# GpSimd's next operation made to depend on a mask or weight-split pass of VectorE, in a cross-attention layer with layer norm

## The chip, the cores and the metric

The kernel runs on one core of a Trainium2 chip. The metric is the device time of one execution in microseconds: before the change the median of 3 runs is 513.0 us (512.81 to 514.88). A core has five engines that work side by side, each through its own queue of instructions in order: TensorE (PE; its weight loads are shown apart as PEld), VectorE (DVE), ScalarE (ACT), GpSimd (POOL) and SyncE (SP), which here only issues DMAs. Engines wait for each other by semaphores. An instruction that waits holds up everything behind it in its engine's queue.

## What is computed

Four sequences of 2048 rows attend to 77 context rows each, 16 heads of 32; the output projection, the residual and a layer norm follow. Everything is float32, and the mask drops the last context rows.

```python
qs = (q @ wq).reshape(Bq, Lq, H, HD).transpose(0, 2, 1, 3)
ks_ = (k @ wk).reshape(Bq, Lk, H, HD).transpose(0, 2, 1, 3)
vs = (v @ wv).reshape(Bq, Lk, H, HD).transpose(0, 2, 1, 3)
scores = jnp.einsum('bhqd,bhkd->bhqk', qs, ks_) / jnp.sqrt(jnp.float32(HD))
scores = jnp.where(mask[:, None, :, :], -jnp.inf, scores)
attn_w = jax.nn.softmax(scores, axis=-1)
attn = jnp.einsum('bhqk,bhkd->bhqd', attn_w, vs)
attn = attn.transpose(0, 2, 1, 3).reshape(Bq, Lq, H * HD)
out = attn @ wo + q
mu = jnp.mean(out, axis=-1, keepdims=True)
var = jnp.mean((out - mu) ** 2, axis=-1, keepdims=True)
return (out - mu) / jnp.sqrt(var + EPS) * gamma + beta
```

## The kernel before

The 8192 rows are 64 tiles of 128 (numbers t), 32 blocks of two tiles (b) and 16 groups of four (g). Large products are made of three passes over values that are split into a rounded part and a rest (`xth` and `xtl`, `wqh` and `wql`, `AH` and `AL`), so a rest has to be computed by a subtraction for each operand.

The order of the whole kernel is written out by hand: the string ORDER is a list of words, and a loop at the end of the kernel issues one step per word. A word is a letter and a number, with a part behind a dot. Each engine gets its instructions in the order of the words; there is no scheduler behind it. Waits are derived from the data: an instruction waits for those that write what it reads, or still use what it overwrites. The words that matter here, with their engine and line:

- VectorE: `F` (L356) and `G` (L368) subtract a rounded weight from the loaded weight, for the value and the output weights, 4 of each; `M` (L386) turns mask bytes into an additive bias, 17 passes, of which M28.4 is that of tiles 28 to 31 and M44.4 that of tiles 44 to 47. All three read and write SBUF alone. `T` (L420) takes the maxima of four heads out of the score banks, `r` (L445) the reciprocal of the sums, `t` (L471) transposes the probabilities, `q` (L290) moves queries out of PSUM, `b` (L529) makes the rest of the attention output, `+` (L561) adds the residual, `s` (L575, L576) takes mean and variance.
- ScalarE: `e` (L435) exponentials of four heads, `i` (L266) rounds the input, `a` (L525) rounds the attention output, `k` (L590) scales a tile for the layer norm.
- GpSimd: `j` (L270) the rest of the input, `n` (L450) divides a tile's probabilities by their sums, `f` (L593) and `)` (L596) multiply by gamma and add beta, `v` (L581 to L584) four small operations that make scale and shift of two tiles out of mean and variance. A `P` word that ends in g is a DMA which GpSimd issues (L482).
- TensorE: `Q` queries, `B` values' projection, `S` scores, `V` probabilities by values, `O` output projection.

A tile goes S, T, e, r, n, t, then by DMA into the layout for V. The probability buffers are three (`pbuf`), the score banks rotate through the eight PSUM banks by a table. So a tile's maxima free the banks for a later tile's scores, and n of a tile has to be done before t can begin. Words that stand close in ORDER on different engines don't run at the same time: each engine comes to its word when its own queue does.

## Time and profile before

| | before |
|---|---|
| median of the runs | 513.0 us |
| the profiled execution | 513.14 us |
| its span, first to last instruction | 511.3 us |
| granted TensorE clock | 0.998 |
| HBM traffic over the span | 115 GB/s |
| VectorE transposes, 64 | 95.8 us busy, 1498 ns each |
| GpSimd's n, 63 | 142.3 us busy, 2261 ns each |
| GpSimd's f and ), 56 of each | 72.1 and 72.0 us busy, 1292 and 1289 ns each |
| GpSimd's j, 28 of one form | 67.4 us busy, 2408 ns each |

The profile shows one execution. Times in its rows are microseconds from the start of the span: a row of the timeline gives start, duration, engine, line, operation, the tiles written and read, and in brackets how long the engine sat idle before it and whose end released it. A group row gives the shortest, median and longest duration of a line's instructions in nanoseconds. A row of the windows gives a stretch, its length, and how much of it an engine was busy.

### The profile page before, as it was taken

The numbers are of one execution on the slowest core, as the hardware profiler recorded it, in microseconds if no ns is written. First come the engines' busy times: TensorE is split into PE (matmuls) and PEld (weight loads), VectorE is DVE, ScalarE is ACT, GpSimd is POOL, SyncE is SP. The second block draws the span as 40 slices with busy tenths as digits, with TensorE's granted clock in tenths as the row PEclk, the third lists the DMA queues.
The fourth block names the chain that finished last, engine by engine and source line by source line (L and its number), as shares of the span: only waits on it lengthen the run. The fifth ranks groups of instructions, "written<-read, shape, count | busy, mean of one in ns | idle before, by whom it ended". The sixth has DMA issues, their size and how long they took to land. (4 is left out here: it accounts for less than half of the span.)

```text
span 511.3 us, 20308 instructions
## 1 busy us (share of the span) xinstructions
PE 499.2 (98%) x6833; PEld 383.9 (75%) x6833; DVE 470.3 (92%) x2563; ACT 464.6 (91%) x2222; POOL 421.1 (82%) x387
## 2 busy tenths in 40 slices
PE   8998999999999999999999999999999999999994
PEld 6976777777777877777777777778777777777773
DVE  5799889988999989988989998999999999999997
ACT  6698999999999999998999999999999999989720
POOL 2556656876897999998898899898999899898896
PEclk9999999999999999999999999999999999999999
DMA  8954786878686986779877868787879677699655
GB/s 307 390 196 131 173 220 163 230 177 225 192 245 182 267 222 169 229 210 249 245 223 210 228 172 252 178 219 204 247 201 235 189 217 240 192 228 252 162 185 216
DMA packets 58781, 110.85 MB, mean 217 GB/s; under 512 B 9462, under 2 KB 11278, under 8 KB 58678
## 3 DMA queue, kind: packets, MB, share of 16 engines
q1 hardware_dynamic: 55222, 102.75, 72.0%
q0 software_dynamic: 2496, 5.77, 4.0%
q8 instruction: 54, 0.88, 0.8%
q10 hardware_dynamic: 960, 1.05, 0.8%
q14 instruction: 49, 0.40, 0.3%
HBM read 41.79 MB, written 16.78 MB: 115 GB/s over the span
## 5 line engine op out<-in xcount | busy, mean ns | idle before, releaser
L435 ACT ACTIVATE pbuf<-pbuf,nm 128x77 f32<-128x77 f32 x1024 | 352.7, 352 | 8.7 <-DVE nm L420 8.0
L435 ACT ACTIVATION_READ_ACCUMULATOR pbuf<-pbuf,nm 128x1 f32 x1024 | 197.1, 193 | 0.0
L420 DVE CUSTOM_DVE_ANT_0 pbuf<-sc,mb 128x77 f32<-128x77 f32 x1024 | 170.0, 231 | 6.4 <-PE sc L403 4.6
L450 POOL TENSOR_TENSOR pbuf<-pbuf,ri 128x1232 f32<-128x1232 f32 x63 | 142.3, 2261 | 34.8 <-DVE ri L445 29.6
L552 PE MATMUL po<-woh,AH 128*128 128x512 f32 x256 | 104.0, 406 | 0.1
L471 DVE STREAM_TRANSPOSE B<-pbuf 128x1280 f32<-128x1280 f32 x64 | 95.8, 1498 | 8.2 <-POOL pbuf L450 7.2
L276 PE MATMUL pq<-xth,wqh 128*128 128x512 f32 (+1 forms) x256 | 100.6, 393 | 0.9 <-DVE nm L420 0.6
L552 PE MATMUL po<-wol,AH 128*128 128x512 f32 x256 | 100.0, 391 | 0.0
L552 PE MATMUL po<-woh,AL 128*128 128x512 f32 x256 | 99.9, 390 | 0.0
L276 PE MATMUL pq<-xtl,wqh 128*128 128x512 f32 (+1 forms) x256 | 98.2, 383 | 0.0
L276 PE MATMUL pq<-xth,wql 128*128 128x512 f32 (+1 forms) x256 | 98.1, 383 | 0.0
L420 DVE DVE_READ_ACCUMULATOR2_ANT nm<- 128x1 f32 x1024 | 84.4, 82 | 0.0
L270 POOL TENSOR_TENSOR xtl<-xtf,xth 128x1024 fp32r<-128x1024 f32 x28 | 67.4, 2408 | 9.6 <-issue 4.8
L593 POOL TENSOR_TENSOR o<-o,gam 128x512 f32<-128x512 f32 x56 | 72.1, 1292 | 2.9 <-ACT o L590 2.7
L596 POOL TENSOR_TENSOR o<-o,bet 128x512 f32<-128x512 f32 x56 | 72.0, 1289 | 1.4
L403 PEld LDWEIGHTS sc<-kct,q 32*64 32x64 f32 x4096 | 51.8, 130 | 24.4 <-issue 11.5
L403 PE MATMUL sc<-kct,q 32*64 32x77 f32 x4096 | 61.7, 238 | 2.2 <-DVE q L290 1.6
L496 PE MATMUL pa<-PT,vsb 96*32 96x256 f32 x992 | 59.7, 382 | 0.0
L552 PEld LDWEIGHTS po<-woh,AH 128*128 128x128 f32 x256 | 48.0, 188 | 15.3 <-issue 3.8
L276 PEld LDWEIGHTS pq<-xth,wqh 128*128 128x128 f32 x256 | 48.1, 188 | 14.7 <-issue 2.1
L552 PEld LDWEIGHTS po<-woh,AL 128*128 128x128 f32 x256 | 48.1, 188 | 10.5
L276 PEld LDWEIGHTS pq<-xth,wql 128*128 128x128 f32 x256 | 48.1, 188 | 9.6
(99 smaller groups left out, 640.3 us busy)
## 6 DMA issues: line engine op xcount, KB each, us to landing
PT<-B SPq DMA_DIRECT2D x343, 128.0 KB
xtf<-xT SPq DMA_DIRECT2D x28, 512.0 KB
o<-x SPq DMA_DIRECT2D x56, 256.0 KB
out<-o SPq DMA_DIRECT2D x56, 256.0 KB
PT<-B POOLq DMA_DIRECT2D x25, 128.0 KB, 4.8
stage_a<-kin SPq DMA_DIRECT2D x4, 410.0 KB
xtf<-xT SPq DMA_DIRECT2D x4, 256.0 KB
wq_f<-wq SPq DMA_DIRECT2D x4, 256.0 KB
```

Of the source, the lines that this page charges most:

```text
L270: nc.gpsimd.tensor_tensor(l[:, c : c + 2], fx.pop((g, c)), xh[g][:, c : c + 2].bitcast(F32), ALU.subtract)
L276: nc.tensor.matmul(pq, w[:, c, m * P : (m + 1) * P], r[g][:, c, rs], start=(n == 0), stop=(n == 11))
L403: mm = nc.tensor.matmul(sc[j][r0 : r0 + SR, g * NK : (g + 1) * NK], qs[q, g, rs.start + r0 : rs.start + r0 + SR], kct[q, g, t // TPB, keys ...
L420: nc.vector.tensor_tensor_reduce(pb[:, h // 2, (h % 2) * NK : (h % 2 + 1) * NK], scs[t][j][:, g * NK : (g + 1) * NK], mb[:, t % TPB, keys_ ...
L435: nc.scalar.activation(pb[:, h // 2, (h % 2) * NK : (h % 2 + 1) * NK], pb[:, h // 2, (h % 2) * NK : (h % 2 + 1) * NK], AF.Exp, bias=nmax[t ...
L450: nc.gpsimd.tensor_tensor(pv, pv, rv.to_broadcast((P, NP, 2, NK)), ALU.mult)
L471: nc.vector.transpose(bt.rearrange("p c q r -> p q c r"), pbuf[t % NPB].rearrange("p q (c r) -> p q c r", c=5),)
L496: nc.tensor.matmul(pas[b, g // 2][HD * j : HD * (j + 1), (g % 2) * BLK : (g % 2 + 1) * BLK], vsb[:, 2 * b // TPB, h % 2, HD * (h // 2) : H ...
L552: nc.tensor.matmul(pos[t], a[:, c, rs], w[:, c, :], start=(first and c == 0 and n == 0), stop=(c == NC_D - 1 and n == 2),)
L593: nc.gpsimd.tensor_tensor(od[t], od[t], gam, ALU.mult)
L596: nc.gpsimd.tensor_tensor(od[t], od[t], bet, ALU.add)
```

## The change

The helpers now return their instruction. While the words of ORDER are issued, the last instruction of a word F, G or M is remembered; the first word j, n, f or ) behind it in ORDER gets a dependency on that instruction, and the memory is cleared. Nothing is computed otherwise and no instruction changes its place on any engine.

```diff
+    def wait_for(later, earlier, reason):
+        info = mybir.DependencyInfo(mybir.DependencyClass.Sync, mybir.DependencyReason.DATA)
+        tc.add_manual_dep(later.ins, earlier.ins.name, info, reason=reason)
...
+    shared = None
     for word in ORDER.split():
...
-            ops[op](int(k or 0), int(part or 0))
+            ins = ops[op](int(k or 0), int(part or 0))
+            if op in "FGM":
+                shared = ins
+            elif shared and op in "jnf)":
+                wait_for(ins, shared, "VectorE's pass over two tiles of SBUF is begun ahead of GpSimd's")
+                shared = None
```

There are 25 words F, G and M, and 16 dependencies, since several passes can stand ahead of one GpSimd word: j2 on M8.4, n0 on F0, j5 on F2, j7 on G0, n9 on M28.4, f2 on M16.4, n14 on M20.4, )2 on M24.4, n24 on M32.4, n30 on M36.4, n35 on M44.4, j23 on M40.4, n45 on M48.4, n47 on M52.4, f45 on M56.4 and )46 on M60.4. A dependency is a wait for the semaphore that VectorE counts up at the end of the pass.

The order in which the instructions stand is unchanged; what changes are the semaphores that GpSimd waits for. GpSimd from the division n35 (of tile 35, in `pbuf_82`) to f25, before:

```order
L450 TENSOR_TENSOR pbuf_82<-pbuf_82,ri_5018 128x8x154 [waits DVE_49]
L596 TENSOR_TENSOR o_4415<-o_4415,bet 128x512
L593 TENSOR_TENSOR o_4542<-o_4542,gam 128x512 [waits DMAHW6_49,Activation_49]
L270 TENSOR_TENSOR xtl_5178<-xtf_2_4894,xth_5008 128x1024 [waits DMAHW7_49,PE_49]
L593 TENSOR_TENSOR o_4530<-o_4530,gam 128x512 [waits Activation_49]
```

and with the change (the lines are 3 further down in the file):

```order
L453 TENSOR_TENSOR pbuf_82<-pbuf_82,ri_5018 128x8x154 [waits DVE_49,Activation_49]
L599 TENSOR_TENSOR o_4415<-o_4415,bet 128x512
L596 TENSOR_TENSOR o_4542<-o_4542,gam 128x512 [waits DMAHW6_49,Activation_49]
L270 TENSOR_TENSOR xtl_5178<-xtf_2_4894,xth_5008 128x1024 [waits DMAHW7_49,DVE_49,PE_49]
L596 TENSOR_TENSOR o_4530<-o_4530,gam 128x512 [waits Activation_49]
```

The fourth row, j23, has a new wait for VectorE (DVE_49). The first, n35, had one already, for the reciprocal `ri_5018`; it now waits for a later count of the same semaphore, that of M44.4, and for ScalarE's exponentials by name, for which the reciprocal stood before. VectorE's own rows from that reciprocal on, the same in both:

```order
L445 RECIPROCAL ri_5018<-sum_4911 128x16
L529 TENSOR_TENSOR AL_5035<-pa_0_4916,AH_5033 128x512
L471 STREAM_TRANSPOSE B_5038<-pbuf_81 128x8x5x32
L561 TENSOR_TENSOR o_4438<-po_5040,o_4438 128x512
L290 COPY q_5073<-pq_3_5060 128x512
L386 TENSOR_SCALAR mb_3681<-m_2_2585 128x384
L529 TENSOR_TENSOR AL_5035<-pa_1_4917,AH_5033 128x512
L471 STREAM_TRANSPOSE B_5038<-pbuf_82 128x8x5x32
```

Between the first row, which n35 waited for, and the sixth, M44.4, for which it waits now, stand four operations of VectorE; the eighth is t35, which waits for n35. The other place is GpSimd's )46 (`o_7660`, adding `bet`) with v24 and three DMA issues ahead of n58, before:

```order
L596 TENSOR_TENSOR o_7660<-o_7660,bet 128x512 [waits Pool_49]
L581 TENSOR_TENSOR rn_8203<-mv_8004,small 128x2 [waits DVE_49]
L582 TENSOR_TENSOR rn_8203<-rn_8203,small 128x2 [waits Pool_49]
L583 TENSOR_TENSOR rn_8203<-mv_8004,rn_8203 128x2 [waits Pool_49]
L584 TENSOR_TENSOR rn_8203<-rn_8203,small 128x2 [waits Pool_49]
L482 DMA PT_8143<-B_8058 32x2x512 [waits DMAHW2_49,DMASW2_49,DMAHW3_49,DMASW1_49,DMAHW6_49,DVE_49,PE_49]
```

and with the change:

```order
L599 TENSOR_TENSOR o_7660<-o_7660,bet 128x512 [waits DVE_49,Pool_49]
L584 TENSOR_TENSOR rn_8203<-mv_8004,small 128x2
L585 TENSOR_TENSOR rn_8203<-rn_8203,small 128x2 [waits Pool_49]
L586 TENSOR_TENSOR rn_8203<-mv_8004,rn_8203 128x2 [waits Pool_49]
L587 TENSOR_TENSOR rn_8203<-rn_8203,small 128x2 [waits Pool_49]
L485 DMA PT_8143<-B_8058 32x2x512 [waits DMAHW2_49,DMAHW3_49,DMASW2_49,DMAHW6_49,DMASW1_49,PE_49]
```

The wait for VectorE has moved from the later rows to )46 itself: M60.4 stands behind everything of VectorE that v24 and the first DMA waited for, so their own waits have gone.

## The prediction

> **What bounds the kernel now.** The first view is the page's busy times, the second the waits of TensorE (engine, what it ran, for whom it waited: us in total, times, longest).

> ```profile
> PE 499.2 (98%) x6833; PEld 383.9 (75%) x6833; DVE 470.3 (92%) x2563; ACT 464.6 (91%) x2222; POOL 421.1 (82%) x387
> PE sc L403 <- DVE q L290: 1.6, 2, 1.3
> PE pq L276 <- DVE nm L420: 0.6, 1, 0.6
> PE sc L403 <- DVE q L292: 0.4, 1, 0.4
> PE sc L403 <- DVE nm L420: 0.2, 1, 0.2
> ```

> TensorE is the bound, and it hardly waits: all that it loses to VectorE in the whole run is 1.6 + 0.6 + 0.4 + 0.2 = 2.8 us. That is the ceiling of any gain from VectorE alone. But the other two engines of the score loop are over 90% busy and are chained to each other by every tile (maxima, exponentials, GpSimd's division, transposition), so an in-order engine that is held for some microseconds has little room to hide it. Small gain, larger risk: the rest works out both.

> The third view is that of the passes on which the change hangs (ns: shortest, median, longest).

> ```profile
> L386 DVE TENSOR_SCALAR mb<-m x17: 204/354/2109, 18.3 to 446.5; 128x384 bf16<-128x384 uint8 x15, 128x96 bf16<-128x96 uint8 x1, 128x288 bf16<-128x288 uint8 x1
> L368 DVE TENSOR_TENSOR wol<-stage_b,woh x4: 673/683/2904, 32.9 to 44.3; 128x512 fp32r<-128x512 f32 x4
> ```

> A mask pass takes 0.35 us and once 2.11; a split takes 0.68 and once 2.90. Each stretched one began while a GpSimd operation ran and ended shortly after it. That stretch is what a different order of the two could give back. I lay the 25 passes and the 16 GpSimd operations that now depend on one of them beside each other by their place in the order. Six waits were fulfilled anyway: those of n0, n9 and n30 stand behind a reciprocal that VectorE does later than the pass, and those of j2, j7 and f45 began after the pass had ended. Ten bind: j5, f2, n14, )2, n24, n35, j23, n45, n47, )46. Four of them are dropped from the sum: f2 goes later, into GpSimd's idle time ahead of n14, and at n14, n24 and n47 the pass is already running when they would begin, so that they lose less than its 0.35 us, and their transpositions are not due yet.

> **Place 1, j5 (gain).** GpSimd's j5, VectorE's G1 and F2 that follow each other, then who waited at the end of it.

> ```profile
> 32.79 2.49 POOL L270 TENSOR_TENSOR xtl<-xtf,xth 128x1024 fp32r<-128x1024 f32 x1 [1.53 <-ACT xth L266]
> 32.93 2.90 DVE L368 TENSOR_TENSOR wol<-stage_b,woh 128x512 fp32r<-128x512 f32 x1
> 35.76 0.68 DVE L356 TENSOR_TENSOR wvlAL<-stage_b,wvh 128x512 fp32r<-128x512 f32 x1
> 40.84 0.36 ACT L435 ACTIVATE pbuf<-pbuf,nm 128x77 f32<-128x77 f32 x1 [3.05 <-DVE nm L420]
> 46.27 0.35 PE L403 MATMUL sc<-kct,q 32*64 32x77 f32 x10 [1.34 <-DVE q L290]
> 41.00:70.00 29.00, 29.00 (x161) 1.00 0.71 165
> ```

> G1 stood behind j5. With j5 waiting for F2, G1 takes 0.68, F2 ends at 34.2 instead of 36.4, and j5 runs from 34.3 to 36.7, 1.5 late; n1 follows it at once, and is not late, since the reciprocal that it waited for comes earlier too. So VectorE is 2.2 us ahead, and about 1.7 ahead after it has waited for n1 and run once against j4. ScalarE's wait of 3.05 shrinks by that; the last row (ScalarE alone, 41 to 70 us) shows it busy for all of the next 29.0 us, so its lead lasts. TensorE's wait of 1.34 at 46.27 goes: **-1.5**, with a little of the next waits for evacuations. Nothing in this stage is late in its place: j5's tile is for the queries of the third group, which TensorE reaches after this wait. Bounds: 0 (the lead is lost later) to -1.8.

> **Place 2, n35 and j23 (loss).** GpSimd's rows n35, )23, f24, j23, )25 and v13, VectorE's M44, t35 and M40, and ScalarE's scaling k27.

> ```profile
> 276.47 2.26 POOL L450 TENSOR_TENSOR pbuf<-pbuf,ri 128x1232 f32<-128x1232 f32 x1
> 278.69 1.29 POOL L596 TENSOR_TENSOR o<-o,bet 128x512 f32<-128x512 f32 x1
> 279.94 1.40 POOL L593 TENSOR_TENSOR o<-o,gam 128x512 f32<-128x512 f32 x1
> 281.31 2.40 POOL L270 TENSOR_TENSOR xtl<-xtf,xth 128x1024 fp32r<-128x1024 f32 x1
> 285.03 1.29 POOL L596 TENSOR_TENSOR o<-o,bet 128x512 f32<-128x512 f32 x1
> 288.17 0.20 POOL L581 TENSOR_TENSOR rn<-mv,small 128x2 f32<-128x2 f32 x1 [1.84 <-DVE mv L576]
> 279.53 0.67 DVE L386 TENSOR_SCALAR mb<-m 128x384 bf16<-128x384 uint8 x1
> 280.72 1.49 DVE L471 STREAM_TRANSPOSE B<-pbuf 128x1280 f32<-128x1280 f32 x1
> 285.39 1.15 DVE L386 TENSOR_SCALAR mb<-m 128x384 bf16<-128x384 uint8 x1
> 288.75 0.49 PE L276 MATMUL pq<-xth,wqh 128*128 128x512 f32 x1 [0.59 <-DVE nm L420]
> 289.72 0.82 ACT L590 ACTIVATE o<-o,rn 128x512 f32<-128x512 f32 x1 [0.40 <-POOL rn L584]
> 290.50:327.40 36.90, 36.74 (x181) 1.00 0.84 218
> ```

> M44 is not moved, and nothing ahead of it on VectorE waits for GpSimd, so it still starts at 279.53; unstretched it ends at 279.86. n35 now runs from 279.95 to 282.2 instead of 276.47 to 278.73: 3.5 us of GpSimd idle. t35 needs n35, and goes from 280.72 to 282.25; VectorE is 1.5 late. M40 comes at 287.0 and ends at 287.35 (0.8 saved, it was stretched to 286.54). In GpSimd's queue stand )23 (to 283.5), f24 (to 284.8) and then j23, which waits for M40: 287.4 to 289.8, 6.1 late. Behind it come f25 and )25, to 292.4, and only then the four small operations of v13, 288.17 to 289.7 before, now 292.4 to 293.95. k27 waits for v13 already now, to the end (0.40): it goes from 289.72 to 294.0, **4.25 late**. Behind it in ScalarE's order are the evacuation that b15.1 on VectorE needs and the exponentials of tiles 37 to 42; the last row (ScalarE alone) shows 36.74 of 36.90 us busy, so nothing of the 4.25 comes back before 327. It reaches TensorE by the next rows: the reciprocal r39 behind the exponentials, n39, t39 directly behind n39, and the scores of tile 42 in the banks that the maxima behind t39 free.

> ```profile
> 311.32 2.25 POOL L450 TENSOR_TENSOR pbuf<-pbuf,ri 128x1232 f32<-128x1232 f32 x1 [0.35 <-DVE ri L445]
> 313.61 1.51 DVE L471 STREAM_TRANSPOSE B<-pbuf 128x1280 f32<-128x1280 f32 x1
> 317.60 0.95 PE L403 MATMUL sc<-kct,q 32*64 32x77 f32 x64
> ```

> n39 ended at 313.57 and t39 began at 313.61: no slack. So I take **+4.2**. Bounds: 0.75 (only TensorE's wait at 288.75 grows, by VectorE's 0.8) to 4.25.

> **Place 3, )46 (loss).** GpSimd's )46, v24's first, three DMA issues and n58; VectorE's M60 and t58; TensorE's S61.

> ```profile
> 442.49 1.30 POOL L596 TENSOR_TENSOR o<-o,bet 128x512 f32<-128x512 f32 x1
> 443.73 0.20 POOL L581 TENSOR_TENSOR rn<-mv,small 128x2 f32<-128x2 f32 x1
> 445.82 1.67 POOL L482 DMA_DIRECT2D PT<-B  x3 [0.54 <-DVE nm L420]
> 447.50 2.27 POOL L450 TENSOR_TENSOR pbuf<-pbuf,ri 128x1232 f32<-128x1232 f32 x1
> 446.50 0.35 DVE L386 TENSOR_SCALAR mb<-m 128x384 bf16<-128x384 uint8 x1
> 450.84 1.50 DVE L471 STREAM_TRANSPOSE B<-pbuf 128x1280 f32<-128x1280 f32 x1
> 457.94 0.95 PE L403 MATMUL sc<-kct,q 32*64 32x77 f32 x64
> ```

> M60 is not stretched, so nothing is to be had. )46 waits for its end at 446.85 and is 4.5 late, v24 ends at 449.7, the three issues take 1.67, n58 runs from 451.4 to 453.65 (3.9 late), and t58 starts at 453.7 instead of 450.84. VectorE is 2.8 late from there through the maxima of tile 60, t59 and the maxima that free banks for tile 61's scores and the product behind them. S61 can start some 1 us late, the product behind it 2.2 late. I take **+2.5**; bounds 0 and 3.9, the delay of n58.

> **The small places.** n45 waits for M48, and )2 for M24; and TensorE's wait at 360.16.

> ```profile
> 349.95 2.26 POOL L450 TENSOR_TENSOR pbuf<-pbuf,ri 128x1232 f32<-128x1232 f32 x1
> 350.31 2.11 DVE L386 TENSOR_SCALAR mb<-m 128x384 bf16<-128x384 uint8 x1
> 360.16 0.31 PE L403 MATMUL sc<-kct,q 32*64 32x77 f32 x6 [0.19 <-DVE nm L420]
> 133.08 1.29 POOL L596 TENSOR_TENSOR o<-o,bet 128x512 f32<-128x512 f32 x1
> 134.74 1.09 DVE L386 TENSOR_SCALAR mb<-m 128x384 bf16<-128x384 uint8 x1
> ```

> M48 falls from 2.11 to 0.35, for a delay of n45 of only 0.8; VectorE gains 1.8 there and the wait at 360.16 goes with what hangs on it: -0.4. At M24 VectorE gains 0.74, while )2 waits until 135.1 and goes 2.0 late with the queue behind it; GpSimd's idle fifth (82% busy) takes up most of that before a transposition is due. I take +0.2, an estimate between -0.7 and +2.0.

> **The sum** is made against the profiled execution, 513.1 us (span 511.3 and 1.8 around it), which is 0.1 above the median of 513.0: 513.1 - 1.5 + 4.2 + 2.5 - 0.4 + 0.2 = 518.1, so **518 us**, 1% slower.

> **The rivals.**
> *Faster: a wait costs the pass alone.* The stretches are worth 2.2 + 0.7 + 0.8 + 0.3 + 1.8 = 5.8 us of VectorE; if GpSimd lost only the passes' own 0.35 to 0.68 us, its idle fifth would cover that, and TensorE could win its 2.8 us: 510.3. For it speaks that VectorE and GpSimd do block each other; against it, that the waits last until VectorE's queue comes to the pass: 3.5, 6.1 and 4.5 us at n35, j23 and )46. [...] M48 against n45 agrees about the blocking, but no row has GpSimd waiting for a pass not yet begun. Chance 0.08.
> *Absorbed.* The waits bind but three score buffers hide most of it: -1.5 - 0.4 + 0.75 + 1 gives 513. Against it speak t39 with no slack and k27, which waits already. That the edit does nothing would end here as well; the added semaphores in the built program speak against that. Chance 0.20.
> *Worse.* Place 1's lead is lost before 280, or place 3 costs all of 3.9: 519.5 to 521.5. For it: 230 us lie between, in which the three engines wait for each other in both directions. Chance 0.14.
> *The forecast*, 515.6 to 519.5: 0.58.

> **How the numbers follow.** The low end takes place 2 at 0.75, place 3 at 0 and the gains whole: 513.1 - 1.5 - 0.4 + 0.75 = 512. The high end is 513.1 + 0.2 + 4.25 + 3.9 = 521.5. About 0.5%, 2.6 us, is what a measurement of this kernel can tell from no change. Faster by more: 0.08; within, 510.4 to 515.6: 0.20; slower by more, the forecast and the worse case: 0.72.

> **What would show it.** Right: G1 at 0.68 and no wait of TensorE near 45; GpSimd idle ahead of n35, j23 and )46; M24, M40, M44 and M48 near 0.35; ScalarE waiting some 4 us for v13 near 290; TensorE's waits on VectorE grown by some 6 us, near 290 to 320 and 455 to 465. Wrong: ScalarE's wait at k27 under 2 us, or t35 and t58 at their old distance from the rows ahead of them.

## The result, and the profile after

The change makes the kernel slower: 519.2 us, median of 4 runs (517.67 to 522.16), against 513.27 of the kernel before on the same chip (4 runs, 512.81 to 514.88). The ratio is 1.0119, 95% interval 1.0082 to 1.0157. The profiled execution took 519.35 us, its span is 517.5 (before 511.3), so 6.2 us are to be found in it.

The lines that answer to those of before: busy times, then waits for VectorE's passes, for GpSimd and by TensorE (engine, what it ran, for whom: us in total, times, longest). The lines of the file are 3 further down.

```profile
PE 502.4 (97%) x6833; PEld 385.7 (75%) x6833; DVE 464.2 (90%) x2563; ACT 464.4 (90%) x2222; POOL 420.3 (81%) x387
```

```profile
DVE B L474 <- POOL pbuf L453: 13.4, 12, 3.3
ACT o L593 <- POOL rn L587: 10.7, 4, 3.9
POOL pbuf L453 <- DVE mb L386: 6.5, 5, 3.5
POOL o L599 <- DVE mb L386: 4.5, 1, 4.5
PE sc L406 <- DVE nm L423: 1.6, 3, 0.9
PE po L555 <- ACT pbuf L438: 1.6, 1, 1.6
PE po L555 <- DVE nm L423: 1.3, 2, 0.9
PE sc L406 <- DVE q L290: 1.1, 1, 1.1
PE sc L406 <- DVE q L292: 0.4, 1, 0.4
PE pq L276 <- DVE nm L423: 0.3, 1, 0.3
```

The first two of these waits as they were before:

```profile
DVE B L471 <- POOL pbuf L450: 7.2, 9, 2.0
ACT o L590 <- POOL rn L584: 4.4, 3, 3.4
```

The passes of VectorE (ns: shortest, median, longest) after:

```profile
L386 DVE TENSOR_SCALAR mb<-m x17: 203/341/409, 18.6 to 449.4; 128x384 bf16<-128x384 uint8 x15, 128x96 bf16<-128x96 uint8 x1, 128x288 bf16<-128x288 uint8 x1
L368 DVE TENSOR_TENSOR wol<-stage_b,woh x4: 679/682/874, 33.2 to 42.7; 128x512 fp32r<-128x512 f32 x4
```

So the change does what it says. The longest mask pass fell from 2.11 to 0.41 us and the longest split from 2.90 to 0.87, and VectorE is busy 6.1 us less (470.3 to 464.2). But other waits have grown: GpSimd now waits for mask passes, 6.5 and 4.5 us in the two largest rows; VectorE's transpositions wait 13.4 us for GpSimd instead of 7.2, and ScalarE's scaling 10.7 instead of 4.4. At the end of these chains TensorE stands: its six rows make 6.3 us (4.7 of them for VectorE), against 2.8 before.

**Where TensorE loses and gains.** I take the start of each tile's scores in the profiled run and subtract the same start of before. The difference is steady over long stretches and steps at few places:

| stretch | after minus before, us | step |
|---|---|---|
| scores of tiles 0 to 4 | +0.2 to +0.3 | start-up |
| tiles 9 to 17 | -1.8 | -2.0 at place 1 |
| tiles 18 to 36 | -2.0, then -1.6 | -0.2, and +0.4 between tiles 22 and 26 |
| tiles 41 to 48 | +3.3 | +4.9 at place 2 |
| tiles 49 to 61 | +2.9 | -0.4 at M48 |
| tiles 62 and 63 | +5.7 | +2.8 at place 3 |
| last product of tile pair 58/59 | +6.3 | +0.6 near 478 |

**Place 1.** GpSimd's j5, then VectorE's G1 and F2, as start, duration, operation:

```profile
34.62 2.41 POOL L270 TENSOR_TENSOR xtl<-xtf,xth 128x1024 fp32r<-128x1024 f32 x1 [3.08 <-ACT pbuf L438]
33.20 0.69 DVE L368 TENSOR_TENSOR wol<-stage_b,woh 128x512 fp32r<-128x512 f32 x1
33.80 0.69 DVE L356 TENSOR_TENSOR wvlAL<-stage_b,wvh 128x512 fp32r<-128x512 f32 x1
```

G1 takes 0.69 instead of 2.90, and j5 begins 0.13 after the end of F2 (34.49). The page names ScalarE as j5's releaser; F2's end is the later one. TensorE's wait of 1.34 at 46.27 has no row any more.

**Place 2.** GpSimd's n35 and j23; VectorE's M44, t35, M40 and b15.1; ScalarE's k27:

```profile
278.41 2.25 POOL L453 TENSOR_TENSOR pbuf<-pbuf,ri 128x1232 f32<-128x1232 f32 x1 [3.49 <-DVE mb L386]
285.87 2.37 POOL L270 TENSOR_TENSOR xtl<-xtf,xth 128x1024 fp32r<-128x1024 f32 x1 [2.71 <-issue]
277.92 0.34 DVE L386 TENSOR_SCALAR mb<-m 128x384 bf16<-128x384 uint8 x1
280.70 1.51 DVE L474 STREAM_TRANSPOSE B<-pbuf 128x1280 f32<-128x1280 f32 x1 [1.83 <-POOL pbuf L453]
285.38 0.35 DVE L386 TENSOR_SCALAR mb<-m 128x384 bf16<-128x384 uint8 x1
293.71 0.69 DVE L532 TENSOR_TENSOR AL<-pa,AH 128x512 fp32r<-128x512 f32 x1 [2.64 <-ACT AH L528]
292.39 0.81 ACT L593 ACTIVATE o<-o,rn 128x512 f32<-128x512 f32 x1 [3.08 <-POOL rn L587]
```

GpSimd stands 3.49 us for a pass of 0.34 and 2.71 us for one of 0.35: not the passes cost, but the time until VectorE's queue comes to them. v13 is late with the queue, ScalarE stands 3.08 us at k27 (0.40 before), and VectorE stands 2.64 us for the evacuation behind k27. k27 starts 2.67 us later than before by the clock of the trace, 4.3 later against the 1.6 us that the kernel was ahead. TensorE at the end of that chain: a product that waits for the maxima behind t35, the scores of tile 40, products of an output projection, the scores of tile 42; then the granted clock in stretches of 3.41 us, as long as the one at 0.50 (stretch, length, TensorE's busy time and number of instructions, clock, DMA share, GB/s):

```profile
283.75 0.47 PE L555 MATMUL po<-woh,AH 128*128 128x512 f32 x1 [0.87 <-DVE nm L423]
...
300.27 0.35 PE L406 MATMUL sc<-kct,q 32*64 32x77 f32 x4 [1.14 <-DVE q L290]
301.00 0.31 PE L406 MATMUL sc<-kct,q 32*64 32x77 f32 x2 [0.38 <-DVE nm L423]
301.63 0.89 PE L406 MATMUL sc<-kct,q 32*64 32x77 f32 x58 [0.32 <-DVE nm L423]
302.46 0.50 PE L555 MATMUL po<-woh,AH 128*128 128x512 f32 x1
...
305.07 0.63 PE L555 MATMUL po<-wol,AH 128*128 128x512 f32 x1
305.50 0.63 PE L555 MATMUL po<-woh,AL 128*128 128x512 f32 x1
...
306.91 0.40 PE L555 MATMUL po<-woh,AH 128*128 128x512 f32 x1
...
320.89 0.95 PE L406 MATMUL sc<-kct,q 32*64 32x77 f32 x64
```

```profile
299.72:303.13 3.41, 2.16 (x67) 1.00 1.03 294
303.13:306.54 3.41, 3.41 (x10) 0.50 0.64 178
306.54:309.95 3.41, 3.41 (x17) 1.00 0.88 238
```

Before, the first and the thirteenth of the same products, and the clock in 2 us of them:

```profile
300.76 0.50 PE L552 MATMUL po<-woh,AH 128*128 128x512 f32 x1
...
303.62 0.39 PE L552 MATMUL po<-woh,AH 128*128 128x512 f32 x1
```

```profile
304.00:306.00 2.00, 2.00 (x11) 1.00 0.91 213
```

Up to k27 the waits are as foreseen; their way on to TensorE and the clock are not. TensorE stands 0.87 us at 283.75, and 1.14, 0.38 and 0.32 at tile 40's scores. Tile 41's scores (315.20, before 311.88) are 3.32 later than before and tile 42's, which have no wait, 3.29 (before 317.60): the loss is complete ahead of them. Behind the three gaps of 1.14, 0.38 and 0.32 us the granted clock falls to 0.50, and the products follow each other every 0.43 us (305.07 to 305.50) instead of every 0.23 (301.32 to 301.55 before). From the first to the thirteenth product of this output projection go 4.45 us (302.46 to 306.91); before it was 2.86 (300.76 to 303.62). So in this profile 1.6 of the 4.9 us of place 2 are the clock's, and the other 3.3 the waits'.

**Place 3.** GpSimd's )46, VectorE's M60 and t58 (which waits for n58), TensorE's gaps:

```profile
449.92 1.28 POOL L599 TENSOR_TENSOR o<-o,bet 128x512 f32<-128x512 f32 x1 [4.54 <-DVE mb L386]
449.40 0.36 DVE L386 TENSOR_SCALAR mb<-m 128x384 bf16<-128x384 uint8 x1
457.16 1.51 DVE L474 STREAM_TRANSPOSE B<-pbuf 128x1280 f32<-128x1280 f32 x1 [3.34 <-POOL pbuf L453]
462.09 0.90 PE L406 MATMUL sc<-kct,q 32*64 32x77 f32 x58 [0.90 <-DVE nm L423]
464.58 0.47 PE L555 MATMUL po<-woh,AH 128*128 128x512 f32 x1 [1.58 <-ACT pbuf L438]
478.36 0.47 PE L555 MATMUL po<-woh,AH 128*128 128x512 f32 x1 [0.41 <-DVE nm L423]
```

M60 gains nothing (0.35 to 0.36), )46 waits 4.54 us for it, VectorE 3.34 for n58, and TensorE loses 0.90 and 1.58, then 0.41. Here the granted clock stays at 1.00 (459 to 468).

### The profile page after: what moved, and what is told of

It reads as the page before. It is cut to its first block, busy times and chain, and to the rows that moved or that the text cites. A ratio compares the mean times of both kernels' runs of the same rounds, so it can differ in the third digit from the quotient of the medians.

```text
span 517.5 us, 20317 instructions
## 1 busy us (share of the span) xinstructions
PE 502.4 (97%) x6833; PEld 385.7 (75%) x6833; DVE 464.2 (90%) x2563; ACT 464.4 (90%) x2222; POOL 420.3 (81%) x387
## 5 line engine op out<-in xcount | busy, mean ns | idle before, releaser
L474 DVE STREAM_TRANSPOSE B<-pbuf 128x1280 f32<-128x1280 f32 x64 | 95.8, 1500 | 16.1 <-POOL pbuf L453 13.4
L276 PE MATMUL pq<-xth,wqh 128*128 128x512 f32 (+1 forms) x256 | 100.6, 393 | 0.6 <-DVE nm L423 0.3
L276 PE MATMUL pq<-xth,wql 128*128 128x512 f32 (+1 forms) x256 | 98.2, 384 | 0.0
L276 PE MATMUL pq<-xtl,wqh 128*128 128x512 f32 (+1 forms) x256 | 98.1, 383 | 0.0
L270 POOL TENSOR_TENSOR xtl<-xtf,xth 128x1024 fp32r<-128x1024 f32 x28 | 67.2, 2399 | 12.3 <-ACT xth L266 6.5
L596 POOL TENSOR_TENSOR o<-o,gam 128x512 f32<-128x512 f32 x56 | 72.1, 1291 | 4.8 <-ACT o L593 2.7
L276 PEld LDWEIGHTS pq<-xth,wqh 128*128 128x128 f32 x256 | 48.1, 188 | 14.3 <-issue 2.5
L555 PEld LDWEIGHTS po<-wol,AH 128*128 128x128 f32 x256 | 48.6, 190 | 9.6 <-issue 0.5
```

Source lines behind the costliest of these rows:

```text
L270: return nc.gpsimd.tensor_tensor(l[:, c : c + 2], fx.pop((g, c)), xh[g][:, c : c + 2].bitcast(F32), ALU.subtract)
L276: nc.tensor.matmul(pq, w[:, c, m * P : (m + 1) * P], r[g][:, c, rs], start=(n == 0), stop=(n == 11))
L474: nc.vector.transpose(bt.rearrange("p c q r -> p q c r"), pbuf[t % NPB].rearrange("p q (c r) -> p q c r", c=5),)
L555: nc.tensor.matmul(pos[t], a[:, c, rs], w[:, c, :], start=(first and c == 0 and n == 0), stop=(c == NC_D - 1 and n == 2),)
L596: return nc.gpsimd.tensor_tensor(od[t], od[t], gam, ALU.mult)
```

## The experiments

The theory from here on: a dependency costs GpSimd the time until VectorE's queue reaches the pass, and the kernel loses where something behind GpSimd's operation was due; TensorE's loss has two parts, its waits and a half clock behind clustered gaps (0.50 for 3.41 us in the profiled run). The rivals: the waits are hidden and the loss is spread over all sixteen; or the clock is an accompaniment that costs nothing.

Most kernels keep only some of the dependencies, by the name of the waiting word:

```diff
+    HELD = ("j5", "n45",)
     shared = None
...
             elif shared and op in "jnf)":
-                wait_for(ins, shared, "VectorE's pass over two tiles of SBUF is begun ahead of GpSimd's")
+                if word in HELD:
+                    wait_for(ins, shared, "VectorE's pass over two tiles of SBUF is begun ahead of GpSimd's")
                 shared = None
```

The medians of before beside them are 513.62 us (17 runs) for e1 to e4, 513.33 (15) for e5 to e8, 513.44 (17) for e9 and e10, 513.25 (11) for e11 and e12.

### e1_gain: the two waits that should pay, alone

The diff above, with j5 and n45.

> Only two of the 16 dependencies are kept, j5 on F2 and n45 on M48.4. Theory (a wait pays where it lets VectorE's pass go first and GpSimd's queue has nothing urgent behind it): TensorE keeps the 2.0 us that it wins near 46 us and the 0.4 near 360, so about 511.0 us, 2.3 below before, and G1 and M48 take 0.69 and 0.36 us. Rival (a lead of VectorE is lost again on the way, the bound is TensorE's own work): 513, the same as before.

Measured: 511.39 us (510.35 to 512.9, 7 runs), ratio 0.996 (0.9945 to 0.9974). Faster than before, by 2.2 us. The gain is there, and two of the sixteen dependencies have it all.

### e2_not_three: all but the three that should cost

```diff
+    HELD = ("j2", "n0", "j5", "j7", "n9", "f2", "n14", ")2", "n24", "n30", "n45", "n47", "f45",)
```

> All dependencies except those of n35, j23 and )46. Theory: as with the two alone, less the 0.4 us that the wait of )2 on M24.4 costs: about 511.4 us. Rival (the harm is spread over all the waits, and the three are only the largest): 514 or more.

Measured: 511.84 us (510.85 to 513.37, 11 runs), ratio 0.9967 (0.9957 to 0.9977). With thirteen dependencies the kernel is as fast as with two, as far as these runs can tell (0.45 us apart at the median), so the loss hangs on n35, j23 and )46 (e3 and e4 keep these alone). "Spread over all sixteen" falls. The step of +0.4 between tiles 22 and 26, some 40 us behind M24, is in e2's profile too (the scores' starts go from -2.1 to -1.6) and not in that of e1, which does not keep the wait of )2 on M24.4.

### e3_place2 and e4_place3: the costly waits, apart

```diff
+    HELD = ("n35", "j23",)
```

> Only n35 on M44.4 and j23 on M40.4. Theory (these two cost what the changed kernel loses between the scores of tile 37 and those of tile 42, 4.9 us in its trace): 517 to 518.5 us, and ScalarE waits some 4 us for v13 ahead of k27. Rival (a third or more of the loss was the lower clock granted to TensorE behind its gap in that one execution): 516 or less in runs whose mean clock is at that of before.

```diff
+    HELD = (")46",)
```

> Only )46 on M60.4. Theory: t58 is 3 to 3.5 us late and nothing of it comes back before the end: 516 to 517 us. Rival (near the end the tail behind TensorE hides part of it): 514.5 or less.

Measured: e3 519.35 us (516.61 to 520.01, 4 runs), ratio 1.0096 (1.0071 to 1.0121); e4 517.5 (516.15 to 518.63, 4 runs), ratio 1.0075 (1.0054 to 1.0095). Both places cost, each more than its term of the sum (4.2 and 2.5) and more than I expected: 5.7 and 3.9 us at the median. But the runs of one kernel differ by more than 2 us: e4 gave 516.15, 516.4, 518.6 and 518.63, e3 once 516.61 and three times over 519. A window of e3's profile shows the granted clock at half:

```profile
304.00:306.00 2.00, 2.00 (x61) 0.50 0.99 274
```

e4's profile was taken of the run of 516.15, with a granted clock of 1.00 through its gaps. Every run also has a mean granted clock on record. It counts the end of the span, which is at half clock in the profiles of before and of the whole change (the last 2.2 of 511.3 and 2.8 of 517.5 us); the runs of the kernel before lie between 0.995 and 0.998, and a stretch of 3.41 us at half takes another 0.0033 (half of 3.41, by 517.5). e3's run of 516.61 had 0.995 and lost 3.0 us; its longer runs had 0.994, 0.990 and 0.989. The rival of e3 named 516 or less, which was not reached, but nearly half of the median's loss is missing in the one run whose clock is that of before. Of e4's two longer runs one had 0.989. The other had 0.995, which can be with or without a stretch at half, so what it lost is open.

### e5_n35 and e6_j23: the two waits of place 2, apart

```diff
+    HELD = ("n35",)
```

> Only n35 on M44.4. Theory (the price is how late a wait makes GpSimd's queue reach the work that others wait for): n35 is 3.5 us late, t35 and VectorE 1.5, v13 and ScalarE's k27 also 1.5; TensorE loses 1.2 to 1.8 us, 515 us. Rival (n35 alone makes most of the loss of the pair, since t35 and t36 hang on it): 517 or more.

```diff
+    HELD = ("j23",)
```

> Only j23 on M40.4. Theory: j23 goes 4.5 us late, v13 and k27 2.6, less than with both; VectorE wins 0.8 at M40.4; TensorE loses 2 to 3 us, 515.5 to 516.5 us. Rival (j23's own product is not due for 20 us, so its delay is harmless): 513 or less.

Measured: e5 513.92 us (513.39 to 516.75, 10 runs), ratio 1.0018 (1.0002 to 1.0034): 0.6 us, less than I expected. e6 516.29 (515.11 to 517.45, 4 runs), ratio 1.0063 (1.0044 to 1.0081): 3.0 us, in the expected range. k27 in e5, then TensorE's longest gap near it:

```profile
291.38 0.82 ACT L593 ACTIVATE o<-o,rn 128x512 f32<-128x512 f32 x1 [0.45 <-POOL rn L587]
```

```profile
285.37 0.47 PE L555 MATMUL po<-woh,AH 128*128 128x512 f32 x1 [0.88 <-DVE nm L423]
```

and k27 in e6:

```profile
292.43 0.81 ACT L593 ACTIVATE o<-o,rn 128x512 f32<-128x512 f32 x1 [3.07 <-POOL rn L587]
```

In e5 ScalarE waits for v13 hardly longer than the 0.40 of before: GpSimd had 1.84 us of idle time ahead of v13, which takes up much of n35's delay. k27 starts 1.66 us later than before (291.38 against 289.72), near the 1.5 that I expected, and TensorE still loses only half of what I expected. What is lost goes another way, by t35 and the maxima behind it, to TensorE's gap of 0.88. In e6 j23 stands directly ahead of f25, )25 and v13, and ScalarE waits 3.07. So it is j23 that makes ScalarE stand. But e6's profile has the half clock too, from some 301.2 to 308.1 (0.81 in 300:302, 0.50 up to 308, 0.98 in 308:310), and three of its four runs have a mean clock of 0.991 or 0.992; the fourth, with 0.995, took 515.11. So j23's wait alone costs at most some 1.8 us, and that e6's median came out in the expected range, which was worked out for the wait alone, is in part the clock's doing.

### e7_k_later: both waits, but ScalarE does not stand there

k27 and k26 go behind the exponentials e38.2; both waits of place 2 stay.

```diff
-... n36 x32 P16.5s k27 a15.1 b15.1 )24 S38 T38.3 T38.1 T38.0 k26 e37.0 T38.2 e38.3 e38.2 r37 ...
+... n36 x32 P16.5s a15.1 b15.1 )24 S38 T38.3 T38.1 T38.0 e37.0 T38.2 e38.3 e38.2 k27 k26 r37 ...
```

> Both dependencies of place 2 (n35, j23), and ScalarE's two scalings k27 and k26, which wait for the late v13, put behind four batches of exponentials (e38.2). Theory (the loss goes through ScalarE, which stands still at k27 while exponentials and an evacuation are ready behind it): b15.1 no longer waits, TensorE's gap near 300 us shrinks by 1 us or more, 515 to 516.5 us. Rival (it goes through GpSimd's divisions to VectorE's t35 and t36, ScalarE only stands by): as with the pair alone, 519.

Measured: 515.66 us (515.55 to 516.42, 5 runs), ratio 1.0054 (1.0041 to 1.0066), 2.3 us over its own kernel before, where e3 with the same two waits lost 5.7. GpSimd's queue is as late as in e3. VectorE no longer waits for b15.1's input, and TensorE's first gap near 300 is gone:

```profile
301.45 0.31 PE L406 MATMUL sc<-kct,q 32*64 32x77 f32 x2 [0.38 <-DVE nm L423]
302.09 0.89 PE L406 MATMUL sc<-kct,q 32*64 32x77 f32 x58 [0.32 <-DVE nm L423]
```

and with it the fall of the clock:

```profile
304.00:306.00 2.00, 2.00 (x11) 1.00 1.00 243
```

So ScalarE's stand makes the gap behind which the clock falls, and the 519 of the rival does not come. Most of the 3.4 us won are the clock's: with the clock held up in another way the two waits still lose 3.0 (e8, the next run), and e7 loses 2.3, so that ScalarE's stand is worth some 0.7 us of the waits. The moved words can have a price of their own; how the 2.3 divide between that and GpSimd's late divisions, this run does not show.

### e8_fill: both waits, and more work for TensorE

To tell the waits from the clock, TensorE is given seven products that nobody uses, ahead of the gaps.

```diff
+    HELD = ("n35", "j23",)
...
             pas[b, i] = bank(f"pa_{b}_{i}")
+        for _ in range(7 if b == 16 else 0):
+            nc.tensor.matmul(pas[b, 0], wqh[:, 0, :P], wqh[:, 0, :], start=True, stop=True)
```

> Both dependencies of place 2, and seven extra products of 128x128 by 128x512 (1.6 us of TensorE) whose result is overwritten at once, ahead of the product of values 16, where TensorE would stand still 1.8 us soon after. Theory of the clock (TensorE's idle time near 300 us is followed by some 4 us at half clock, and that makes 1.5 to 2.5 us of the loss): with the gap filled the clock stays at 1.00 from 302 to 308 us and the time falls to 516.5 to 517.5 in spite of the added work. Rival (the low clock has another cause, or costs nothing since the other engines are late anyway): 519 or more.

Measured: 516.32 us (515.68 to 516.5, 5 runs), ratio 1.0061 (1.0049 to 1.0074): a loss of 3.0 us where e3 lost 5.7, with 1.6 us more of products. Two rows show why: the products stand where TensorE was idle, and the clock does not fall (1.00 from 294 to 312).

```profile
298.61 1.90 PE L497 MATMUL pa<-wqh 128*128 128x512 f32 x7
...
303.06 0.89 PE L406 MATMUL sc<-kct,q 32*64 32x77 f32 x58 [0.32 <-DVE nm L423]
```

```profile
304.00:306.00 2.00, 2.00 (x9) 1.00 0.77 218
```

The runs lie within 0.8 us of each other instead of 3.4. So the waits of place 2 cost 3.0 us (516.32 less 513.33), as much as e3's shortest run lost (516.61 less 513.62), and the other 2.7 of e3's median go with the clock at least in part. In e3's profiled run, which has some 3.4 us at half clock (0.86, 0.50 and 0.79 in 302:304, 304:306 and 306:308), place 2 takes 4.7 us by the scores' starts; 1.0 more between tiles 49 and 50 and 0.5 near 478 are not explained. "The clock costs nothing" falls at this place.

### e9_moved and e10_moves_alone: move the pass, not GpSimd

The theory says what would be better: a pass should stand where GpSimd idles anyway. M24.4 goes behind M16.4, M40.4 and M44.4 behind M36.4, F0 behind I0 (the diff shows where they now stand); e9 keeps j5's and n45's dependencies too, e10 none.

```diff
-... T1.2 e0.3 F0 T1.3 I0 e1.2 ...
+... T1.2 e0.3 T1.3 I0 F0 e1.2 ...
-... t13 M16.4 T16.1 ...
+... t13 M16.4 M24.4 T16.1 ...
-M36.4 a12.1 b12.1 ...
+M36.4 M40.4 M44.4 a12.1 b12.1 ...
...
+    HELD = ("j5", "n45",)
```

> Only the waits at j5/F2 and n45/M48.4 are kept; besides, four passes stand elsewhere in VectorE's order, where GpSimd idles: mask M24.4 behind M16.4, masks M40.4 and M44.4 behind M36.4, copy F0 behind I0. Theory (each pass costs TensorE where ScalarE or GpSimd is next late): the gap of 0.6 us at 288.75 and about 0.4 us near 28.8 go besides what e1_gain saved, so 510.3 to 510.8 us. Rival (TensorE's own work is the bound once the gap at 46 is gone, or VectorE is late near 243 in their place): 511.4 us as in e1_gain, or more.

> No wait of the change is kept; only the four passes are moved as in e9_moved. Theory: the gaps at 28.8 and 288.75 go, the one at 46 stays: 512.3 to 512.8 us, 0.5 to 1 us under the kernel before. Rival (the passes cost as much where they stand now): no change from the kernel before, 513.3 us.

Measured: e9 510.47 us (509.68 to 511.09, 6 runs), ratio 0.9936 (0.9918 to 0.9954); e10 512.26 (511.43 to 513.97, 12 runs), ratio 0.9976 (0.9963 to 0.9988). Both as the theory had it, e10 just past the end of its range: the moves alone give 1.2 us, with the two waits 3.0. What each of the four moves gives was not measured apart. e9 is the fastest kernel of the study, faster than the kernel before and than the one with the change. Three mask passes in a row in e9, where GpSimd waits 3.02 us for a reciprocal anyway:

```profile
240.81 0.85 DVE L386 TENSOR_SCALAR mb<-m 128x384 bf16<-128x384 uint8 x3
```

```profile
242.50 2.26 POOL L453 TENSOR_TENSOR pbuf<-pbuf,ri 128x1232 f32<-128x1232 f32 x1 [3.02 <-DVE ri L448]
```

Three passes take 0.85 us together, and after the start (1.2 us, as before) TensorE waits for VectorE once more, for 0.8 us:

```profile
PE po L555 <- DVE nm L423: 0.8, 1, 0.8
```

### e11_fill3 and e12_after_fill: the clock at place 3, and in the whole change

e4's and the whole change's kernel with the seven products of e8 ahead of the block product V27 (near 453); e12 has them ahead of V16 too.

```diff
+        for _ in range(7 if b == 27 else 0):
+            nc.tensor.matmul(pas[b, 0], wqh[:, 0, :P], wqh[:, 0, :], start=True, stop=True)
```

> As e4_place3 (only )46 waits), with seven more products of 128x128 by 512 columns (1.6 us of TensorE, results overwritten) ahead of V27, the last product of a block ahead of the gaps of 0.85 and 1.55 us near 460. e4_place3 gave 516.15, 516.4, 518.6 and 518.63. Theory (the two long runs lost their 2.3 us to the half clock behind these gaps, as at place 2): the gaps shrink by 1.6 together, TensorE's end stays as in e4's short runs, all runs 516 to 517, median 516.3. Rival (the long runs have another reason, or TensorE has no room here): median 517.5 or more, runs still 2 us apart.

> The whole change, with seven such products ahead of V16 (near 298) and seven ahead of V27 (near 454). The whole change gave 519.2 (517.67 to 522.16). Theory (its waits cost about 3.1 at place 2, 2.8 to 3.4 at place 3, less 2.0 at place 1; the rest is the half clock): 516.5 to 517.5, in spite of 3.2 us more work of TensorE. Rival (the clock plays no part): 519.2 or, with the added work, up to 522.

Measured: e11 516.44 us (516.11 to 516.84, 6 runs), ratio 1.0056 (1.004 to 1.0073). No run over 516.84, where two of e4's four were at 518.6: with the products that fill the gaps there were no long runs, and the mean clock of all six is 0.996 or 0.997. For e4's long run with 0.989 that speaks for the clock; no profile of a long run was taken, and the cause of the one with 0.995 stays open (e5 had such a run too, 516.75 with 0.995). e12 518.19 us (517.81 to 518.59, 6 runs), ratio 1.009 (1.0071 to 1.0108): the runs draw together (0.8 us instead of 4.5) and the median falls by 1.0, but it stays above the 516.5 to 517.5 that I expected. Its mean clocks are 0.996 and 0.997. The four runs of the whole change had 0.986 (522.16 us), 0.994 (519.35 and 519.06) and 0.996 (517.67): the lower the clock, the longer the run, and the one at 0.996 is as short as e12's. What was left shows near the end, where the next block's probabilities are late and TensorE waits for their DMA:

```profile
480.46 1.93 PE L501 MATMUL pa<-PT,vsb 96*32 96x256 f32 x32 [1.03 <-DMA PT<-B]
```

With the whole change this product starts at 481.29 without a wait of its own. So it may be that a part of what the half clock takes at place 2 is not lost twice, since the chain of the other engines is late there anyway and a TensorE that comes earlier waits; no run tests this.

## Why the prediction was right, and where its sizes were off

The forecast was 518.0 us, the time is 519.2, and sign, places and, as far as ScalarE, the chain are as foreseen. Point by point:

- **Place 1**, -1.5 in the sum, measured -2.0 in the profile; e1, with j5 and n45, is 2.2 faster at the median. Mis-sized: I left room for what would be lost between n1 and the maxima, and little was.
- **Place 2**, +4.2 in the sum, by way of v13 and k27. Up to ScalarE the chain is right: k27 is 4.3 late where I wrote 4.25, and e5 and e6 find j23 as the wait behind ScalarE's stand. The step that failed is the one from ScalarE to TensorE. The sum let the whole 4.25 arrive at tile 42's scores by way of r39, n39 and t39, since t39 has no slack. The trace has the loss complete at tile 41, in two pieces that the sum had no term for: 0.87 us at 283.75 for the maxima behind the late t35 (e5 has it with n35 alone), and the gaps of 1.14, 0.38 and 0.32 at tile 40's scores, the first of which e7 removes by letting b15.1 go ahead. The waits cost 3.0 (e8), not 4.2. That the place came out near its term owes to what the sum did not have: the half clock behind the gaps, 1.6 us in the profiled run; e3's median lies 2.7 above the loss of the waits. The right total of this place is in part a coincidence.
- **Place 3**, +2.5, measured 2.8 and 0.6 in the profile, 3.2 in e11 (516.44 less 513.25). Mis-sized: the wait came to 1.58 at the product and again 0.41 at 478, within the bound of 3.9.
- **M48**, -0.4, measured -0.4; **M24**, +0.2, measured +0.4; the six fulfilled waits and the four small ones, nothing that e2 can tell.
- **The sum of the waits alone**: -2.0 + 3.0 + 3.2 = +4.2 by the parts, +4.9 by e12 (518.19 less 513.25). The forecast had +5.0. What the parts lack of the whole, 0.7, may be e12's wait of 1.03 at 480.46, which e11's trace does not have; that is not shown.
- **The signs**: G1, the mask passes and GpSimd's idle times came as named. ScalarE's wait at k27 is 3.08 us, short of "some 4" and over the 2 that would have been wrong. TensorE's waits grew by 3.5 us (2.8 to 6.3), by 1.9 for VectorE alone, and not by "some 6": at half clock TensorE loses time while it counts as busy (3.41 of 3.41 us at 0.50, from 303.13), and its busy time rose by 3.2 (499.2 to 502.4).
- **The rival "a wait costs the pass alone"** is out for n35, j23 and )46: GpSimd stood 3.49, 2.71 and 4.54 us for passes of 0.34 to 0.36. The block that spoke for it is seen in VectorE's passes: the four of the mask that were stretched take 0.32 to 0.36 us instead of 0.67 to 2.11. The order was turned, and the block went; the price of the turning is the time until VectorE's queue comes to the pass. Where the pass was already running or next in line the rival was right: at n45 GpSimd stood 0.82 us and VectorE gained 1.75.
- **"Absorbed" and "worse"** did not come at the median, though one run took 522.16; e5 is a small case of the first: n35's wait alone costs 0.6 us, since GpSimd's idle time ahead of v13 takes up half of its 3.5 us.

## What to carry to other kernels

The dependency between two in-order queues cost here from when the one was ready until the other's queue reached the operation, whatever that operation's own length (3.49, 2.71 and 4.54 us for passes of 0.34 to 0.36): price it by the distance in the queue, and by what stands behind the waiting instruction (here the scaling that ScalarE waits for). If two engines are to be kept apart, move the short pass to where the other engine idles, as e9 does (510.47 us against 513.44), and add a wait only where the pass is next in line anyway (0.82 us at n45). Where a change opens several gaps of TensorE close together, look at the granted clock behind them (0.50 here, behind 1.14, 0.38 and 0.32 us) before the whole loss is put down to the waits.

## What was not expected of the hardware

In the clock records of the whole change's profiled run 296.96 us at 1.00 are followed by 3.41 at 0.50 and 208.21 at 1.00; in that of before the clock is at 1.00 for 505.17 us. The three long stretches are 87, 61 and 148 times the 3.41 us of the one at half (296.96 / 87 = 3.4133, 208.21 / 61 = 3.4133, 505.17 / 148 = 3.4133). By the windows' mean clocks it stays at half for some 3.4 us in e3 and some 6.8 in e6. What sets these lengths is not shown, nor why runs of one kernel differ in their clock as those of e3 do. TensorE's busy time just ahead does not decide alone: it was busy 2.16, some 1.8 and 1.95 of the 3.41 us ahead of the three falls (the whole change, e3 and e6; for the last two by the gaps in the timeline), but 1.95 of 3.41 at place 3 in the whole change (460.14 to 463.55) and 1.74 of 4.00 there in e4 (458 to 462) brought none. What else decides, these runs do not settle.
